# Layer norms of a four-layer graph kernel: centring and scaling on ScalarE, tile by tile, in place of VectorE

## Chip, cores and metric

The kernel runs on one core of a Trainium2 chip. The metric is the device time of one execution in microseconds (us), median of several runs. Profiles are taken in runs of their own, and they take longer: the profiled execution of the kernel before has a span of 7481.3 us, while its plain runs take 5338.69 us. Times inside a profile are therefore used for durations, order and waits, not as shares of the plain time.

## The reference, cut to what matters

Sixteen graphs (B = 16) of 1024 nodes with 64 features go through four layers, and each ends in a layer norm over the 64 features:

```python
def _layernorm(x, axis=-1, eps=1e-5):
    m = jnp.mean(x, axis=axis, keepdims=True)
    v = jnp.var(x, axis=axis, keepdims=True)
    return (x - m) / jnp.sqrt(v + eps)
...
x = _layernorm(x + _L0_gnn_ref(...))   # messages adj @ h, a small tanh MLP
x = _layernorm(x + _L1_gnn_ref(x, adj))  # messages by the row-normalised adjacency
x = _layernorm(x + _L2_gnn_ref(x, adj, nodemask, ...))  # quantiles over a thinned neighbour list, then a relu MLP
x = _layernorm(x + _L3_gnn_ref(x, adj, nodemask, ...))  # the same with other weights
```

So a norm is taken 16 x 4 = 64 times, each over a [128 partitions, 8 tiles, 64 features] float32 tile: 1024 nodes as 8 tiles (NT = 8) of 128 partitions, C = 64.

## The kernel before

The program is made of Python generators that emit instructions. For each graph b, `features` computes layers 0 and 1 (two norms), `lists` the neighbour lists, `ordered` an order of the nodes by list length. For each round k, `sort_round` sorts the gathered neighbour features of two graphs at once (graph k in layer 2, graph k-2 in layer 3), `fill` produces the last tile's neighbours by matmuls with one-hot matrices, and `finish` does the MLP and the norm of layers 2 and 3. The order on each engine is fixed when the program is built. A generator yields a number of microseconds, and it goes on when a clock has moved by that much. The clock is the time of VectorE, counted by a wrapper around its calls:

```python
class Metered:
    def __init__(self, engine):
        self.engine, self.us = engine, 0.0
    def __getattr__(self, name):
        ...
            self.us += 0.13 + size / (3840 if fast else 960)
            return call(*args, **kwargs)
...
    def settle(dst, y, chain):           # the layer norm: y in, dst out
        st = s.work.tile([P, 4, NT], F32, name=f"ln_st_{chain}", bufs=1)
        dve.reduce_sum(st[:, 0], y, axis=AX.X)
        dve.tensor_scalar(st[:, 1], st[:, 0], 1.0 / C, None, op0=ALU.mult)
        dve.tensor_sub(y, y, st[:, 1, :, None].to_broadcast([P, NT, C]))
        yield 2
        nc.scalar.activation(dst, y, AF.Square)
        yield 7
        dve.reduce_sum(st[:, 2], dst, axis=AX.X)
        yield 1
        nc.scalar.activation(st[:, 3], st[:, 2], AF.Sqrt, bias=eps, scale=1.0 / C)
        yield 6
        dve.reciprocal(st[:, 0], st[:, 3])
        dve.tensor_mul(dst, y, st[:, 0, :, None].to_broadcast([P, NT, C]))
```

Where the norm is called, and what follows it:

```python
    def features(b, e):                  # layers 0 and 1
        ...
        yield 8
        for h in range(NH):              # two halves
            ...                          # yields of 50 in each half
            dve.tensor_add(y[:, h * G : (h + 1) * G], pd, x_s[:, h * G : (h + 1) * G])
        dve.tensor_add(y, y, b02r[:, None, :].to_broadcast([P, NT, C]))
        yield from settle(x1[:, :, :C], y, "x")
        while b and not entries[b - 1].packed:
            yield 2
        near = s.sets.tile([P, NT, N], F16, name="near")
        for h in range(NH):
            ...  # matmuls pa <- adj, x1; near = adj > 0
        e.near = near                    # lists(b) starts from this
        ...
        yield from settle(x2, y, "x")
        ...
    def finish(b, e, layer, agg):        # layers 2 and 3
        ...
        yield from settle(xn, y, "m")
        yield 1
        ...
        for t in range(NT):
            put = nc.gpsimd.indirect_dma_start(...)   # one scatter a tile, table<-x3s or out<-agg
    ...
    def prepare():
        for b in range(B):
            while b > allowed[0] or (b and not entries[b - 1].taken):
                yield 2
            preparing[b] = [weave.add(features(b, entries[b]))]
            while b and not entries[b - 1].listed:
                yield 2
            preparing[b].append(weave.add(lists(b, entries[b])))
    ...
        for k in range(B + 2):
            allowed[0] = k + 2
            sort_round(k)
```

In `lists(b)` the flag `taken` is set after the last write of the tile `takes`, which is where `features(b + 1)` may start. The first instruction of `features` on VectorE sets a column of x1 to 1 (a MEMSET on x). The weighted sum over sorted neighbours already runs on ScalarE with a per-partition factor, one 128x64 tile at a time:

```python
                nc.scalar.activation(prods[:, m, i, :], got[:, m, slot_id, :], AF.Copy, scale=e.wts[:, t, i : i + 1])
```

The program also holds a general path for graphs whose lists are longer than usual, with a layer norm of its own. It doesn't run on these inputs and isn't changed.

Of the kernel before, what the change touches and what calls it, by code (L numbers as in the profile page):

```python
# [17 lines left out]
AF = mybir.ActivationFunctionType  # L18
ALU = mybir.AluOpType
AX = mybir.AxisListType  # L20

P = 128
# [190 lines left out]
def adj_resnorm_kernel(ctx: ExitStack, tc: tile.TileContext, x, adj_t, nodemask, w01, b01, w02, b02,  # L213
                       w21, b21, w22, b22, w31, b31, w32, b32, out):
    nc = tc.nc
    B, N, C = x.shape
    NT = N // P
# [4 lines left out]
    dve = Metered(nc.vector)  # L222
# [138 lines left out]
    def settle(dst, y, chain):  # L361

        st = s.work.tile([P, 4, NT], F32, name=f"ln_st_{chain}", bufs=1)
        dve.reduce_sum(st[:, 0], y, axis=AX.X)
        dve.tensor_scalar(st[:, 1], st[:, 0], 1.0 / C, None, op0=ALU.mult)
        dve.tensor_sub(y, y, st[:, 1, :, None].to_broadcast([P, NT, C]))
        yield 2
        nc.scalar.activation(dst, y, AF.Square)
        yield 7
        dve.reduce_sum(st[:, 2], dst, axis=AX.X)  # L370
        yield 1
        nc.scalar.activation(st[:, 3], st[:, 2], AF.Sqrt, bias=eps, scale=1.0 / C)
        yield 6
        dve.reciprocal(st[:, 0], st[:, 3])
        dve.tensor_mul(dst, y, st[:, 0, :, None].to_broadcast([P, NT, C]))

    def split(xc, parts, rest):

# [13 lines left out]
    def features(b, e):  # L392
# [18 lines left out]
        for h in range(NH):  # L411
# [26 lines left out]
# [5 lines that stand above are left out]
# [19 lines left out]
        x2 = s.feat.tile([P, NT, C], F32, name="x2", tag="x_s", bufs=1)  # L462
        dve.tensor_add(y, y, x1[:, :, :C])
        yield from settle(x2, y, "x")
        nc.sync.dma_start(table[0][b % 3][:N, :].rearrange("(t p) c -> p t c", p=P), x2)
        while b >= 2 and not entries[b - 2].filled[0]:
# [282 lines left out]
    def finish(b, e, layer, agg):  # L749
# [25 lines left out]
        dve.tensor_add(y, y, xc)  # L775
        xn = agg if layer else s.feat.tile([P, NT, C], F32, name="x3s", bufs=3)
        yield from settle(xn, y, "m")
        yield 1
        dst, rows = (out_rows_of, e.out_rows) if layer else (table[1][b % 3], e.rows)
# [447 lines left out]
```

## Time and profile before

| | |
|---|---|
| time, median of 3 runs | 5338.69 us (5337.18 to 5345.71) |
| span of the profiled execution | 7481.3 us |
| instructions | 107026 |
| instructions of VectorE / ScalarE | 9407 / 4644 |
| busy: TensorE / VectorE / ScalarE / GpSimd | 3981.8 / 4695.2 / 1972.5 / 3369.5 us |

In the profile DVE is VectorE, ACT is ScalarE, PE is the matrix engine and PEld its weight loads, POOL is GpSimd. A group of instructions has its line in the program (L207 is the wrapper through which most of VectorE's calls go, so these are told apart by their tiles), its tiles as output<-inputs, its shapes, its count, busy time, mean duration in ns, and the idle time of the engine before it with what ended that idle time. "remote" stands for a releaser that the trace doesn't name.

### The profile page before, as it was taken

The page shows a single profiled execution, that of the slowest core. Times are in us where ns is not written, and L with a number is a line of the kernel's source. Part 1 is how long each engine was busy: PE and PEld are TensorE (multiplying, and loading weights), DVE is VectorE, ACT ScalarE, POOL GpSimd, SP SyncE. Part 2 cuts the span into 40 slices and gives each one's busy share as a digit, 9 for nine tenths or more (in the row PEclk, how much of TensorE's full clock was granted, in tenths as well). Part 3 has the DMA queues.
Part 4 walks back from the last instruction along what each step waited for, and adds up shares of the span by engine and source line. Part 5 has one row for each costly group of instructions (what it writes and reads, how often), then busy time and mean ns, then how long its engine had stood idle before and what let it go on. Part 6 is the DMA issues. An engine that isn't in the chain of part 4 may idle for free.

```text
span 7481.3 us, 107026 instructions
## 1 busy us (share of the span) xinstructions
PE 3981.8 (53%) x43144; PEld 2843.2 (38%) x43144; DVE 4695.2 (63%) x9407; ACT 1972.5 (26%) x4644; POOL 3369.5 (45%) x3228
## 2 busy tenths in 40 slices
PE   7554566565645546565454655546565563533233
PEld 5333344443434334344243443434344342322232
DVE  2554567758648475675656657675665766558676
ACT  3130423332304132241412323142231413111111
POOL 0425245555533545444354544444545444554352
PEclk8675767676767667676676766666675766655555
DMA  3112111111111111111111111111111110100000
GB/s 83 41 33 46 32 41 39 44 43 41 42 37 30 30 38 39 40 39 42 22 39 30 41 41 34 43 28 29 41 38 45 27 40 14 21 18 15 12 19 10
DMA packets 420585, 259.11 MB, mean 35 GB/s; under 512 B 106590, under 2 KB 368878, under 8 KB 420078
## 3 DMA queue, kind: packets, MB, share of 16 engines
q0 software_dynamic: 102400, 105.06, 7.3%
q1 hardware_dynamic: 317678, 147.12, 7.1%
q8 instruction: 339, 5.55, 0.3%
q14 instruction: 168, 1.38, 0.1%
HBM read 239.37 MB, written 12.58 MB: 34 GB/s over the span
## 4 chain that ended last, share of the span: by engine, by line
DVE 33%; PE 29%; issue 24%; another core or an unknown queue 7%; ACT 3%; POOL 3%; DMA 1%; SPq 0%; DVEq 0%; POOLq 0%; ACTq 0%
DVE other L207 12%; PE pgk L348 10%; DVE got L207 6%; DVE got_s L207 6%; PE pk L592 6%; PE px L420 3%; PE pr L506 2%; POOL got_s L352 2%; PE pa L451 2%; DVE hot L207 2%; PE ordered_x L348 2%; DVE best L207 1%; DVE y_x L207 1%; DVE near L207 1%
## 5 line engine op out<-in xcount | busy, mean ns | idle before, releaser
L352 POOL DMA_INDIRECT got_s<-table,idx x2944 | 3090.2, 1050 | 3714.1 <-DVE other L207 1226.8
L348 PEld LDWEIGHTS <-hot 128*128 128x128 bf16 x24576 | 1141.3, 113 | 1992.0 <-issue 1660.9
L207 DVE TENSOR_SCALAR hot<-place 128x1024 bf16<-128x1024 f16 x1024 | 444.8, 435 | 1406.5 <-remote 1096.8
L348 PE MATMUL pgk<-x3p,hot 128*128 128x64 bf16 x12288 | 726.2, 219 | 865.6 <-issue 693.7
L348 PE MATMUL pgk<-x2p,hot 128*128 128x64 bf16 x12288 | 686.6, 213 | 739.9 <-issue 639.4
L592 PE MATMUL pk<-near,order 128*128 128x512 f16 x2048 | 585.4, 431 | 203.0 <-issue 186.2
L207 DVE TENSOR_TENSOR other<-got_s 128x512 f32<-128x512 f32 (+8 forms) x900 | 514.9, 583 | 12.3 <-DVE got_s L207 0.3
L207 DVE TENSOR_TENSOR got_s<-got_s 128x384 f32<-128x384 f32 (+7 forms) x918 | 490.6, 537 | 18.8
L506 PE MATMUL pr<-steps,near 128*128 128x512 bf16 x1536 | 429.2, 436 | 136.6 <-ACT junk L512 78.3
L737 ACT ACTIVATE got_s<-got_s,wts 128x64 f32<-128x64 f32 x1568 | 398.7, 335 | 290.1 <-DVE got_s L207 258.4
L451 PE MATMUL pa<-x,adj_r 128*128 128x65 f32 x2048 | 404.9, 367 | 118.1 <-issue 84.3
L451 PEld LDWEIGHTS pa<-x,adj_r 128*128 128x128 f32 x2048 | 385.2, 283 | 128.2 <-issue 93.0
L549 PE MATMUL pv<-minus_n,takes 128*128 128x128 bf16 x1024 | 237.7, 257 | 336.4 <-DVE takes L207 331.3
L207 DVE TENSOR_TENSOR got_s<-other 128x512 f32<-128x512 f32 (+8 forms) x774 | 408.0, 540 | 7.2
L592 PEld LDWEIGHTS <-order 128*128 128x128 bf16 x2048 | 208.3, 106 | 534.8 <-issue 365.5
L207 DVE MAX8 best<-code 128x8 f16<-128x1024 f16 x112 | 136.7, 1221 | 409.8 <-ACT code L603 383.5
L727 ACT COPY got<-pgk 128x512 f32<-128x512 f32 x128 | 74.7, 583 | 1125.7 <-remote 534.0
L207 DVE TENSOR_TENSOR other<-got 128x128 f32<-128x128 f32 (+5 forms) x270 | 233.1, 880 | 173.8 <-ACT got L727 165.3
L207 DVE TENSOR_TENSOR other<-other 128x128 f32<-128x128 f32 (+13 forms) x558 | 318.1, 570 | 14.8
L548 PE MATMUL pv<-scaled,near 128*128 128x128 f16 x1024 | 238.8, 258 | 156.2 <-ACT near L553 149.9
L512 ACT ACTIVATE junk<-pr,nb_st 128x1024 f16<-128x1024 f32 x256 | 282.3, 1109 | 149.1 <-PE pr L506 82.6
L549 PEld LDWEIGHTS <-takes 128*128 128x128 bf16 x1024 | 117.9, 115 | 515.7 <-DVE takes L207 355.4
(195 smaller groups left out, 6627.1 us busy)
## 6 DMA issues: line engine op xcount, KB each, us to landing
adj_r<-in_adj_dram SPq DMA_DIRECT2D x256, 512.0 KB
got_s<-table,idx POOLq DMA_INDIRECT x2944
x_s<-in_x_dram SPq DMA_DIRECT2D x16, 256.0 KB
table<-x SPq DMA_DIRECT2D x16, 256.0 KB
x<-table SPq DMA_DIRECT2D x16, 256.0 KB
table<-x3s,rows POOLq DMA_INDIRECT x128
out_dram<-agg,out_rows POOLq DMA_INDIRECT x128
table<-no_row SPq DMA_DIRECT2D x6, 0.2 KB
```

What stands on the lines that cost most here:

```text
L207: return call(*args, **kwargs)
L348: nc.tensor.matmul(dst, hot[:, c, :], parts[:, c, q, :], start=first and c + q == 0, stop=c == NT - 1 and q == 2)
L352: nc.gpsimd.indirect_dma_start(out=dst, out_offset=None, in_=tab, in_offset=bass.IndirectOffsetOnAxis(ap=rows, axis=0))
L420: nc.tensor.matmul(px[C:, q * P : (q + 1) * P], x_s[:, jt, :], adj[t][:, jt, :], start=jt == 0, stop=jt == NT - 1)
L451: nc.tensor.matmul(pa[:, q, :], adj[i][:, jt, :], x1[:, jt, :], start=jt == 0, stop=jt == NT - 1)
L506: nc.tensor.matmul(pr[:, h * HALF : (h + 1) * HALF], near[:, c, t * P : (t + 1) * P], steps[:, ONSET + h * HALF - c * P :][:, :HALF], star ...
L512: nc.scalar.activation(junk, prs[t - 1], AF.Sign, bias=lim[:, i, t - 1 : t], scale=-1.0, accum_out=cut_at[:, i, t - 1 : t])
L548: nc.tensor.matmul(pv[:, cols], near[:, c, rows], scaled[:, c, :], start=True, stop=False)
L549: nc.tensor.matmul(pv[:, cols], takes[:, c, rows], minus_n, start=False, stop=False)
L592: nc.tensor.matmul(cols, order[:, c, t * P : (t + 1) * P], left(c, slice(h * G, (h + 1) * G)), start=c == 0, stop=c == NT - 1)
L727: nc.scalar.copy(got[:, m, g : g + 8, :], pg)
L737: nc.scalar.activation(prods[:, m, i, :], got[:, m, slot_id, :], AF.Copy, scale=e.wts[:, t, i : i + 1])
```

## The change

Both passes of the norm that combine a whole tile with a per-row number leave VectorE. ScalarE does them instead, with one instruction for each of the 8 tiles: it adds minus the mean as a per-partition bias (Identity), and multiplies by the reciprocal deviation as a per-partition scale (Copy). VectorE keeps the two sums, the mean and the reciprocal. The purpose is to take work from VectorE and give it to an engine with more idle time. The yields are set anew: the wait before the second sum goes from 7 to 9, and a yield of 1 before and of 7 after the scaling are added.

```diff
         st = s.work.tile([P, 4, NT], F32, name=f"ln_st_{chain}", bufs=1)
         dve.reduce_sum(st[:, 0], y, axis=AX.X)
-        dve.tensor_scalar(st[:, 1], st[:, 0], 1.0 / C, None, op0=ALU.mult)
-        dve.tensor_sub(y, y, st[:, 1, :, None].to_broadcast([P, NT, C]))
+        dve.tensor_scalar(st[:, 1], st[:, 0], -1.0 / C, None, op0=ALU.mult)
         yield 2
+        for t in range(NT):
+            nc.scalar.activation(y[:, t, :], y[:, t, :], AF.Identity, bias=st[:, 1, t : t + 1])
         nc.scalar.activation(dst, y, AF.Square)
-        yield 7
+        yield 9
         dve.reduce_sum(st[:, 2], dst, axis=AX.X)
         yield 1
         nc.scalar.activation(st[:, 3], st[:, 2], AF.Sqrt, bias=eps, scale=1.0 / C)
         yield 6
         dve.reciprocal(st[:, 0], st[:, 3])
-        dve.tensor_mul(dst, y, st[:, 0, :, None].to_broadcast([P, NT, C]))
+        yield 1
+        for t in range(NT):
+            nc.scalar.activation(dst[:, t, :], y[:, t, :], AF.Copy, scale=st[:, 0, t : t + 1])
+        yield 7
```

## The prediction

> **What bounds the kernel now.** I began with the page's first part, the busy times:
>
> ```profile
> PE 3981.8 (53%) x43144; PEld 2843.2 (38%) x43144; DVE 4695.2 (63%) x9407; ACT 1972.5 (26%) x4644; POOL 3369.5 (45%) x3228
> ```
>
> The shares are of the profiled span of 7481.3 us. The plain run takes 5338.69 us. VectorE's durations hardly vary from instance to instance (691 to 694 ns for one form below), so I take its busy time to be the same in a plain run: 4695.2 / 5338.69 = 88%. No other engine comes near it by this reckoning except TensorE (75%, with ends that are modelled). Where are the other 5338.7 - 4695.2 = 643 us? I cut the profile into three stretches (columns after the window's length: busy time and instructions of PE, PEld, DVE, ACT, POOL, then granted clock, share of DMA, GB/s):
>
> ```profile
> 0.00:1015.00 1015.00, 579.61 (x5208) 408.36 (x5209) 474.38 (x1220) 275.27 (x528) 325.55 (x355) 0.69 0.19 46
> 1015.00:6356.00 5341.00, 2983.14 (x32582) 2125.19 (x32581) 3473.90 (x6594) 1520.14 (x3542) 2534.77 (x2383) 0.67 0.15 36
> 6356.00:7481.00 1125.00, 419.04 (x5356) 309.63 (x5356) 746.87 (x1595) 177.13 (x574) 509.20 (x491) 0.57 0.08 16
> ```
>
> In the first stretch, until three graphs are prepared, VectorE idles for 541 us; in the last, with nothing left to prepare, for 378. Both are waits on dependencies, part of which a plain run has too. If it keeps some two thirds of them (my guess), about 600 of the 643 idle us lie there, and in the middle VectorE is busy nearly throughout. In the profile it idles in the middle as well. The waits of VectorE between 2700 and 6310 us say on what:
>
> ```profile
> DVE hot L207 <- remote: 634.0, 53, 48.4
> DVE hot L207 <- PE pgk L348: 141.4, 53, 21.4
> DVE best L207 <- ACT code L603: 100.1, 7, 54.2
> ```
>
> `hot` is a one-hot matrix for the fill; its buffer is freed by a matmul, so these are waits on TensorE. TensorE's own largest wait in the whole profile is "issue" (1794.9 us before weight loads), which I read as mostly profiling's own cost, since the plain run is 2142 us shorter. None of these waits has anything to do with the norms. So the middle is bound by VectorE in a plain run, and VectorE's work there is what counts.
>
> **What the skill says.** The Trainium skill, "Perfetto Trace Analysis", section "Optimizing Scalar/DVE Operations": if VectorE is saturated, moving work to ScalarE may make sense; both pay a fixed cost per instruction. "ScalarE: Activation LUTs", section "What ACT_TABLE_LOAD costs": an activation with immediates takes 186 ns + 0.833 ns per element, each per-partition pointer operand adds about 93 ns, and back-to-back activations overlap by about 93 ns. For 64 elements that is 186 + 53 + 93 = 332 ns, one every 239 ns. The trace has the same operation, the weighing with a per-partition factor, and agrees: mean 335 ns, and the median distance from one start to the next is 239 ns. "ScalarE: Activation LUTs", section "Table sets: the hidden batching unit": copy and identity are in every table set, so they cause no table load. The trace agrees for Copy and Square: of 52 loads, 26 stand at the square root and 25 at tanh, one at another line. Identity isn't in the trace.
>
> **The change part by part.** The groups by form, with mean ns after the busy time:
>
> ```profile
> L207 DVE TENSOR_TENSOR y_x<-y_x,ln_st_x 128x512 f32<-128x512 f32 x32 | 22.2, 693 | 1.1
> L207 DVE TENSOR_TENSOR y_m<-y_m,ln_st_m 128x512 f32<-128x512 f32 x32 | 22.2, 693 | 1.1
> L207 DVE TENSOR_TENSOR x<-y_x,ln_st_x 128x512 f32<-128x512 f32 x32 | 22.1, 692 | 1.1
> L207 DVE TENSOR_TENSOR agg<-y_m,ln_st_m 128x512 f32<-128x512 f32 x16 | 11.1, 692 | 0.5
> L207 DVE TENSOR_TENSOR x3s<-y_m,ln_st_m 128x512 f32<-128x512 f32 x16 | 11.1, 692 | 0.6
> ...
> L737 ACT ACTIVATE got_s<-got_s,wts 128x64 f32<-128x64 f32 x1568 | 398.7, 335 | 290.1 <-DVE got_s L207 258.4 <-DVE hot L207 23.8 <-issue 4.0
> ```
>
> Removed from VectorE: 32 + 32 + 32 + 16 + 16 = 128 instructions, 22.2 + 22.2 + 22.1 + 11.1 + 11.1 = 88.7 us busy, and 4.4 us of gaps before them (34 ns each): 93 us, or 1.45 us a norm. A full round has four norms: 5.8 us of its 312 us of VectorE work (distance between the same points of neighbouring rounds, added up in VectorE's busy time).
>
> Added to ScalarE: 64 x 16 = 1024 instructions at 239 ns, 245 us. It then has some 2217 us, 42% of a plain run. In a full round that is 15 us more, on an engine with about 124 us of work in such a round. It is not the bound.
>
> Latency of a norm. The last one of the program, where nothing else is in the way (VectorE and ScalarE lines of the timeline: start, duration):
>
> ```profile
> 7462.42 0.69 DVE L207 TENSOR_REDUCE ln_st_m<-y_m 128x8 f32<-128x512 f32 x1
> 7463.14 0.17 DVE L207 TENSOR_SCALAR ln_st_m<-ln_st_m 128x8 f32<-128x8 f32 x1
> 7463.35 0.69 DVE L207 TENSOR_TENSOR y_m<-y_m,ln_st_m 128x512 f32<-128x512 f32 x1
> 7464.07 0.63 ACT L368 ACTIVATE agg<-y_m 128x512 f32<-128x512 f32 x1 [5.62 <-DVE y_m L207]
> 7464.73 0.69 DVE L207 TENSOR_REDUCE ln_st_m<-agg 128x8 f32<-128x512 f32 x1 [0.70 <-ACT agg L368]
> 7465.46 0.30 ACT L372 ACTIVATE ln_st_m<-ln_st_m,eps 128x8 f32<-128x8 f32 x1 [0.76 <-DVE ln_st_m L207]
> 7465.79 0.20 DVE L207 RECIPROCAL ln_st_m<-ln_st_m 128x8 f32<-128x8 f32 x1 [0.37 <-ACT ln_st_m L372]
> 7466.03 0.69 DVE L207 TENSOR_TENSOR agg<-y_m,ln_st_m 128x512 f32<-128x512 f32 x1
> ```
>
> Each 0.72 us step (0.69 and a gap) becomes eight activations, 7 x 0.239 + 0.335 = 2.0 us. So a norm gets 2 x (2.0 - 0.72) = 2.6 us longer where it is waited for: at the end of the program once (+2.6), and at its start, where VectorE idles and the first graphs' two norms are in the chain: three graphs, at most 3 x 2 x 2.6 = 15 us, of which I count 10.
>
> Lead of the preparation. The yields of a norm go from 2 + 7 + 1 + 6 = 16 to 2 + 9 + 1 + 6 + 1 + 7 = 26. The first norm of `features` lies in a loop: `taken` of graph b, features of b + 1 up to near, lists of b + 1, its `taken`. From the MEMSET that opens `features` to the next such MEMSET, in VectorE's busy time, the trace gives 285, 299 and 290 us for the early graphs and 312 for the late ones. Early, it follows the last `takes` at once (start 2323.94, MEMSET 2326.48); late, it comes 16 us after (4984.86, 5000.83). So early on the loop itself sets the pace (about 290), it gains on the rounds (312), and from the ninth graph or so the limit of two rounds' lead holds it. After the change the loop takes about 290 + 10 (yields) + 2 (lag of two more steps) - 1.45 = 301, the rounds 312 - 5.8 = 306. The preparation still keeps up, but only just: its lead stays small for the whole run rather than growing.
>
> Sum: of the 64 norms I leave out ten as not in a stretch that VectorE bounds (the first three graphs' six in `features` and two in layer 2, the last two of the program). 54 x 1.45 = -78. Start +10, end +2.6. For the smaller lead, with more waits on late lists and on ScalarE's queue, +18 (a guess: 1.5 us for each of 12 rounds). Together -47 us, 5338.7 - 47 = 5291, say 5290.
>
> **The rivals.** (1) TensorE is the bound in the middle: then the 78 us turn into longer waits of `hot`, and the time is 5340 to 5355. For it speaks that `hot` is VectorE's largest wait in the profile; against it that this profile slows TensorE and that the plain run leaves at most some tens of us of idle time in the middle. (2) The preparation loop becomes the bound: if the loop takes 5 us more than a round, 13 x 5 = 65 us are lost again, and the time is about 5340 to 5390. For it speaks the narrow gap of 301 to 306; against it that both are worked out from the same clock. (3) ScalarE's order: its queue is in order, and the scaling can stand behind a copy that waits for a matmul (waits of 10 us and more on TensorE are in its list of waits, 520.9 us in all on pgk alone). VectorE's multiply didn't stand behind those. Then PE's pa matmuls or the scatters come late; the added yield of 7 should cover most of it: +0 to +40. (4) Everything converts: -93 + 5, 5251.
>
> **Range and chances.** Between (4) and the mixed cases: 5230 to 5350. Faster by over 2% would be below 5232, more than the removed work: 0.05. Slower by over 2% would be above 5445, for which the loop would have to lose 13 x 12 us or more: 0.05. Within 2%: 0.90.
>
> **What would show it.** Right: the five groups above are gone, 9407 - 128 = 9279 instructions on VectorE, its busy time about 89 us less; 1024 more activations at 335 ns, one every 239; no more table loads at Identity; the late rounds about 306 us of VectorE's time apart, with the MEMSET right behind the last `takes` throughout. Wrong: VectorE waits for ScalarE at ln_st for more than a few us in many norms; the sort waits for gathers or for the fill more often; VectorE's busy time falls but its idle time before `hot` grows as much; or a VectorE that is not the bound at all, with a time that stays.

## The result, and the profile after

The changed kernel takes 5320.66 us (median of 4 runs, 5318.06 to 5321.83), the kernel before beside it 5342.08 us (5337.18 to 5345.71). The ratio is 0.996, with a 95% interval of 0.9943 to 0.9977. So the change gives 21 us, where the prediction said 48, with the time inside the range of 5230 to 5350. A second comparison gave 0.9961 (0.9946 to 0.9976).

Some of the comparisons, and the profile on which the prediction was built, fell in a condition in which the kernel before takes 7430 to 7624 us in place of 5333 to 5347; the matmuls of the fill then follow each other at about 91 ns in the mean, otherwise at about 51 (distances of up to some 2 us counted), and as one chip showed both, the words "fast chip" and "slow chip" in the expectations below mean this condition. Every ratio here is taken within one comparison. Below, "at 5340" and "at 7480" name the condition by the time of the kernel before.

A new profile of the kernel before, at 5340, has these busy times (first part of the page):

```profile
PE 3434.8 (64%) x43144; PEld 2655.5 (50%) x43144; DVE 4690.2 (88%) x9407; ACT 1969.4 (37%) x4644; POOL 3666.5 (69%) x3228
```

The changed kernel beside it, in the same comparison:

```profile
PE 3377.1 (64%) x43144; PEld 2582.0 (49%) x43144; DVE 4605.8 (87%) x9279; ACT 2208.6 (42%) x5662; POOL 3668.3 (69%) x3228
```

The spans are 5331.5 and 5317.1 us. VectorE has the 128 instructions fewer and 84.4 us less to do. Its idle time, span less busy time, went from 641.3 to 711.3 us: 70 us up. So the work did go, and most of it came back as waiting. ScalarE's 239 us more come with the new groups, of which four are (group, count, busy time, mean ns, idle time before them):

```profile
L368 ACT ACTIVATE y_x<-y_x,ln_st_x 128x64 f32<-128x64 f32 x256 | 64.6, 335 | 315.2 <-DVE ln_st_x L207 315.2
L368 ACT ACTIVATE y_m<-y_m,ln_st_m 128x64 f32<-128x64 f32 x256 | 64.6, 334 | 145.3 <-DVE ln_st_m L207 145.3
L378 ACT ACTIVATE x<-y_x,ln_st_x 128x64 f32<-128x64 f32 x256 | 64.5, 334 | 148.7 <-DVE ln_st_x L207 101.2 <-DVE nb_st L207 47.4
L378 ACT ACTIVATE x3s<-y_m,ln_st_m 128x64 f32<-128x64 f32 x128 | 32.2, 335 | 12.8 <-DVE ln_st_m L207 12.5
```

Where did the waiting come back? Cut into start, middle and end at the same times (columns as in the prediction), the kernel before at 5340:

```profile
0.00:1150.00 1150.00, 772.67 (x8599) 583.82 (x8600) 830.90 (x1907) 429.20 (x889) 588.86 (x579) 0.76 0.24 58
1150.00:4170.00 3020.00, 2086.23 (x26535) 1615.41 (x26532) 2825.95 (x5361) 1239.17 (x2890) 2296.56 (x1967) 0.76 0.23 53
```

and the changed kernel:

```profile
0.00:1150.00 1150.00, 738.29 (x8339) 559.56 (x8340) 783.46 (x1817) 450.41 (x1034) 566.72 (x557) 0.76 0.23 57
1150.00:4170.00 3020.00, 2070.71 (x26595) 1572.58 (x26591) 2805.56 (x5347) 1392.69 (x3549) 2322.11 (x1988) 0.76 0.23 53
```

In the start VectorE works 783.5 us of the 1150 rather than 830.9. In the middle it idles for 214 rather than 194 us. By the rounds (a round ends with VectorE's last sum from the tail tile `got` into `agg`): the first two end at 387 and 695 us before and at 385 and 695 us after, so nothing is lost up to there. The third ends at 1076 before and at 1099 after. The fourth makes up for that (it ends at 1414 and 1413), the fifth loses it again (1716 and 1747). The waits of VectorE between 700 and 1100 us, in the third round, name what was lost there. The kernel before has

```profile
DVE best L207 <- ACT code L603: 10.1, 3, 6.9
...
DVE near L207 <- DMA adj_r<-in_adj_dram: 0.8, 1, 0.8
```

and the changed kernel

```profile
DVE near L207 <- DMA adj_r<-in_adj_dram: 33.7, 1, 33.7
DVE y_m L207 <- PE pd L775: 12.2, 1, 12.2
```

A single instruction on `near`, which compares a block of the adjacency with zero, waits 33.7 us for its load. The program fixes VectorE's order, so the sorting that stands behind this instruction waits too. Neither the norm nor ScalarE is part of this wait. Late rounds, on the other hand, do what the change is for: the last three before the tail take 310.3 to 310.5 us before and 303.5 to 304.1 after.

The fifth round has no such wait. In it VectorE waits for the fill: before, once for 3.5 us, and after the change above all in these places:

```profile
DVE hot L207 <- PE pgk L348: 20.7, 6, 6.9
DVE other L207 <- ACT got L731: 10.2, 1, 10.2
```

Over the whole program the waits show both. Of VectorE's waits in the kernel before, these are

```profile
DVE other L207 <- ACT got L727: 102.9, 14, 10.7
...
DVE near L207 <- DMA adj_r<-in_adj_dram: 42.8, 5, 32.1
DVE hot L207 <- PE pgk L348: 42.5, 34, 5.2
DVE other L207 <- DMA got_s<-table,idx: 33.8, 1, 33.8
DVE y_m L207 <- PE pd L771: 32.7, 5, 13.0
```

and in the changed kernel

```profile
DVE near L207 <- DMA adj_r<-in_adj_dram: 84.1, 5, 39.9
DVE hot L207 <- PE pgk L348: 82.8, 51, 6.9
DVE other L207 <- ACT got L731: 64.3, 14, 10.2
DVE y_m L207 <- PE pd L775: 50.8, 12, 12.2
...
DVE other L207 <- issue: 28.8, 1, 28.8
```

Of the 70 us, 41 are waits of `near`. `hot` waits 40 us more for matmuls of the fill, but `other` waits 39 us less for the copy `got` of what the fill made, so the two together hardly change (145.4 and 147.1 us): the fill is waited for at another place, not longer. The MLP's sum `y_m` waits 18 us more.

Why is the load late? The timeline of the loads' queue (start, time from the first to the last of the merged entries, line, transfer, count) in the kernel before:

```profile
656.27 126.31 SPq L403 DMA_DIRECT2D adj_r<-in_adj_dram  x13
815.84 0.37 SPq L795 DMA_DIRECT2D x<-table  x1
816.31 3.64 SPq L403 DMA_DIRECT2D adj_r<-in_adj_dram  x3
```

and in the changed kernel:

```profile
656.62 113.92 SPq L407 DMA_DIRECT2D adj_r<-in_adj_dram  x9
816.27 0.37 SPq L799 DMA_DIRECT2D x<-table  x1
816.74 19.27 SPq L407 DMA_DIRECT2D adj_r<-in_adj_dram  x7
```

The entry x<-table is the read-back of x3: `read_back`, a generator that `finish` starts after the norm of layer 2, and which the prediction never looked at. It waits until the scatters of x3s have landed (45.7 us in the changed kernel), and loads behind it on the queue wait with it. It goes at 816 us in both kernels. What differs is its place: before, 13 of a graph's 16 loads stood ahead of it, after the change 9. GpSimd's timeline in the changed kernel shows why it goes at 816 us and not earlier (start, duration, what ended the idle time before it):

```profile
803.82 0.94 POOL L352 DMA_INDIRECT got_s<-table,idx  x1 [0.30 <-DMA got_s<-table,idx]
805.07 1.00 POOL L785 DMA_INDIRECT table<-x3s,rows  x1 [0.30 <-DMA got_s<-table,idx]
...
814.02 0.97 POOL L785 DMA_INDIRECT table<-x3s,rows  x1 [0.30 <-issue]
```

The scatters stand behind a run of gathers that began at 728 us. ScalarE had x3s ready by 765.5 us:

```profile
763.50 2.02 ACT L378 ACTIVATE x3s<-y_m,ln_st_m 128x64 f32<-128x64 f32 x8
```

So x3s lay there for 40 us, then the scatters took 10 us, the read-back went, the load behind it went, and `near` started at 821.7 us.

### The profile page after: what moved, and what is told of

It is laid out like the page before. It is cut to its first block, busy times and chain, and to the rows that moved or that the text cites. A ratio compares the mean times of both kernels' runs of the same rounds, so it can differ in the third digit from the quotient of the medians.

```text
span 5320.1 us, 107953 instructions
## 1 busy us (share of the span) xinstructions
PE 3372.3 (63%) x43084; PEld 2586.5 (49%) x43144; DVE 4606.9 (87%) x9279; ACT 2208.3 (42%) x5662; POOL 3671.4 (69%) x3228
## 4 chain that ended last, share of the span: by engine, by line
DVE 69%; PE 14%; POOL 5%; issue 5%; ACT 3%; DMA 3%; DVEq 0%; POOLq 0%; SPq 0%; ACTq 0%
DVE other L207 22%; DVE got_s L207 17%; DVE got L207 10%; DVE hot L207 5%; POOL got_s L352 4%; DVE best L207 4%; PE pgk L348 3%; PE pk L596 3%; PE pa L455 3%; DMA got_s<-table,idx 2%; DVE less L207 2%; PE px L424 1%; PE ordered_x L348 1%; DVE y_m L207 1%; DVE y_x L207 1%
## 5 line engine op out<-in xcount | busy, mean ns | idle before, releaser
L352 POOL DMA_INDIRECT got_s<-table,idx x2944 | 3351.9, 1139 | 1419.5 <-issue 770.8
L348 PEld LDWEIGHTS <-hot 128*128 128x128 bf16 x24576 | 997.8, 110 | 682.5 <-DVE hot L207 568.2
L348 PE MATMUL pgk<-x3p,hot 128*128 128x64 bf16 x12288 | 553.4, 211 | 253.3 <-DVE hot L207 252.7
L348 PE MATMUL pgk<-x2p,hot 128*128 128x64 bf16 x12288 | 550.1, 211 | 213.4 <-DVE hot L207 202.5
L207 DVE TENSOR_TENSOR other<-got_s 128x512 f32<-128x512 f32 (+8 forms) x900 | 516.0, 584 | 49.2 <-issue 28.8
L596 PE MATMUL pk<-near,order 128*128 128x512 f16 x2048 | 473.7, 385 | 20.6 <-ACT code L607 13.9
L510 PEld LDWEIGHTS <-near 128*128 128x128 f16 x1536 | 169.6, 113 | 556.4 <-issue 447.0
L762 PE MATMUL pt<-ident,agg 128*64 128x128 f32 x256 | 52.8, 344 | 488.1 <-DVE agg L207 462.9
L424 PE MATMUL px<-adj_r,x_s 128*64 128x128 f32 x2048 | 270.4, 290 | 13.4 <-DMA adj_r<-in_adj_dram 11.4
L741 ACT ACTIVATE got<-got,wts 128x64 f32<-128x64 f32 x672 | 164.7, 335 | 270.6 <-DVE got L207 270.6
L762 PEld LDWEIGHTS pt<-ident,agg 128*64 128x64 f32 x256 | 29.5, 135 | 500.6 <-DVE agg L207 459.6
```

Source lines behind the costliest of these rows:

```text
L348: nc.tensor.matmul(dst, hot[:, c, :], parts[:, c, q, :], start=first and c + q == 0, stop=c == NT - 1 and q == 2)
L352: nc.gpsimd.indirect_dma_start(out=dst, out_offset=None, in_=tab, in_offset=bass.IndirectOffsetOnAxis(ap=rows, axis=0))
L424: nc.tensor.matmul(px[C:, q * P : (q + 1) * P], x_s[:, jt, :], adj[t][:, jt, :], start=jt == 0, stop=jt == NT - 1)
L510: nc.tensor.matmul(pr[:, h * HALF : (h + 1) * HALF], near[:, c, t * P : (t + 1) * P], steps[:, ONSET + h * HALF - c * P :][:, :HALF], star ...
L596: nc.tensor.matmul(cols, order[:, c, t * P : (t + 1) * P], left(c, slice(h * G, (h + 1) * G)), start=c == 0, stop=c == NT - 1)
L762: nc.tensor.transpose(pt[:C, q * P : (q + 1) * P], agg[:, h * G + q, :], ident)
```

## The experiments

The theory when they began (A): VectorE is the bound, its time does come through, and the missing half is lost at the start and the end. The rival (B): another engine shares the bound in the middle. A third (C) grew out of the traces: the change moves what it doesn't touch, the order on the load queue. The fourth (D) is that the longer lead costs, or that ScalarE's passes do.

**The kernel before again.** No edit. One measurement is at 7480, one at 5340; the latter is the profile used above.

> The kernel before once more, for a profile that isn't stretched as its first one (span 7481 us) was. All theories: span near its plain time, 5337 to 5347 us; VectorE busy about 4695 us. Theory A (VectorE sets the pace, the missing half is lost at the start and the end): a late round takes 309 to 311 us against 303.8 after the change, and the start and the end are some 30 us shorter than after the change. Theory B (another engine shares the bound in the middle): a late round takes about 305 us, with more idle time of VectorE than after the change, and start and end are alike.

Measured: 7508.43 us, VectorE busy 4695.3 us.

> The kernel before once more. The chips differ: it took 5340 us on one and 7480 us on another, where matmuls of the fill follow each other at 91 ns in the mean (after the change, on the faster chip: 49 ns). If this is a fast chip: VectorE busy 4695 us of about 5340, and theory A wants late rounds of 309 to 311 us (303.8 after the change), with a start and an end some 30 us shorter than after the change; theory B wants late rounds of about 305 us. If it is a slow one: again 7450 to 7520 us.

Measured: 5333.27 us, span 5331.5, VectorE busy 4690.2; late rounds 310.3 us. That is A's number for the late rounds, but only half of A's claim: start and end are not 30 us shorter than after the change, the loss begins in the third round. The two profiles together also show that VectorE's busy time doesn't depend on the condition (4695.3 and 4690.2).

**Both passes left out, and given to nobody.** What leaves a norm in this kernel is the square of its input, and centring and scaling are not computed.

```diff
-        dve.tensor_sub(y, y, st[:, 1, :, None].to_broadcast([P, NT, C]))
...
-        dve.tensor_mul(dst, y, st[:, 0, :, None].to_broadcast([P, NT, C]))
```

> Both passes left out and given to nobody, yields as before (what leaves a norm is then the square of its input). Theory A: the middle gives 54 x 1.45 = 78 us and start and end some more: 5245 to 5270 us. Theory B: TensorE or the order of the gathers takes over, and most of the 93 us turn into waits: 5305 to 5325 us.

Measured at 7480: 7366.92 against 7479.84 us, 0.9834 (0.9807 to 0.9861). The expected times were written for 5340 and don't apply.

> Both passes left out, yields as before. On a fast chip: theory A (VectorE's time converts) 5245 to 5270 us; theory B (most of it turns into waits) 5305 to 5325 us. On a slow chip 1.7% below the kernel before, as measured there.

Measured at 5340: 5281.00 against 5339.26 us, 0.9887 (0.9872 to 0.9902). That is 58 us, between both theories. Its waits in the third round:

```profile
DVE near L207 <- DMA adj_r<-in_adj_dram: 42.5, 1, 42.5
DVE best L207 <- ACT code L601: 8.9, 3, 6.9
```

With ScalarE untouched, no yield changed and nothing but VectorE's work gone, the same wait is there, with 11 loads ahead of the read-back. 58 us gained and up to 42 that this one wait takes make about 100 us; the removed work was put at 93, and without the passes the norms in the chain at the start are shorter too (the first round ends at 371 us, before at 387). So apart from the wait VectorE's time seems to have come through, and nothing is left for B to explain at 5340. That is worked out, not shown: the passes left out together with a free load queue were not measured.

**The yields alone.** VectorE does both passes as before.

```diff
-        yield 7
+        yield 9
...
         dve.reciprocal(st[:, 0], st[:, 3])
+        yield 1
         dve.tensor_mul(dst, y, st[:, 0, :, None].to_broadcast([P, NT, C]))
+        yield 7
```

> The kernel before with the yields of the changed kernel (9 for 7, 1 and 7 more), VectorE still does both passes. If the longer lead is what eats the gain: 5360 to 5375 us. If the yields cost nothing: 5335 to 5350 us.

Measured at 7480: 7677.72 us, 1.0255 (1.0230 to 1.0280), far more than expected.

> The kernel before with the yields of the changed one. On a fast chip: 5360 to 5375 us if the longer lead eats the gain, 5335 to 5350 us if it costs nothing there because TensorE has time to spare. On a slow chip 2.5% above the kernel before, as measured there.

Measured at 5340: 5374.23 us, 1.0059 (1.0045 to 1.0073), 35 us slower, at the number of "the longer lead eats the gain". The trace has 28.8 us in the same wait of `near` in the third round (9 loads ahead of the read-back), so a part of the price of the lead is a price of the queue. How large a part this run doesn't show: the third round takes 25 us more than in the kernel before, the fourth 19 less, the fifth 18 more.

**The changed kernel beside them.** No edit.

> The changed kernel itself on this chip. On a fast chip 0.994 to 0.998 of before, as measured. On a slow chip: yields alone cost 2.5% there and leaving the passes out gives 1.7%, the sum is about +1%: 7520 to 7580 us against 7480.

Measured at 5340: 5319.75 us, 0.9961. Leaving out (-58) and the yields (+35) add up to -23, the kernel has -20. That leaves 3 us for ScalarE's passes, but both parts hold the same wait once each and the kernel holds it once, so the small remainder proves little.

**ScalarE's passes with the old yields.** The changed kernel with 7 for 9 and without the yields around the scaling. All four measurements are at 7480 or above; how this version does at 5340 is not known.

```diff
-        yield 9
+        yield 7
...
-        yield 1
         for t in range(NT):
             nc.scalar.activation(dst[:, t, :], y[:, t, :], AF.Copy, scale=st[:, 0, t : t + 1])
-        yield 7
```

> The changed kernel with the yields of the kernel before (7, and none around the scaling). If the longer lead is what eats the gain: 5285 to 5305 us. If ScalarE's longer passes themselves do (in its queue or in waits for it): 5315 to 5335 us, with more waits of VectorE and TensorE for ScalarE at the norms.

> The changed kernel with the yields of the kernel before. Its loads of the adjacency stand in the kernel before's order around the read-back of x3 (13 ahead of it, 3 behind, in the third round; after the change 9 and 7). On a fast chip (before 5340 us): if the order on the load queue is what eats the gain, the third round has no wait of near on adj_r and the time is 5245 to 5275 us; if ScalarE's passes themselves cost, 5290 to 5320 us. On a slow chip (7480 us): 1.003 to 1.008 of before, as measured there.

> The changed kernel with the yields of the kernel before, for a fast chip: 13 loads ahead of the read-back as before, so 5245 to 5275 us if the order on the load queue eats the gain; 5290 to 5320 us if ScalarE's passes do. On a slow chip (7480 us) 1.005 to 1.007 of before, as measured there twice.

> The changed kernel with the yields of the kernel before, in the condition in which before takes 5340 us: its load queue has 13 loads ahead of the read-back, as before, so the third round has no wait of near on adj_r and the time is 5260 to 5290 us; 5300 to 5325 us if ScalarE's passes without a longer lead make VectorE or TensorE wait for them. Where before takes 7480 us: 1.005 to 1.007 of it, as measured there twice.

Measured: 1.0055 (1.0031 to 1.0080), 1.0072 (1.0047 to 1.0098), 1.0051 (1.0033 to 1.0069) at 7480, and 1.0132 (1.0109 to 1.0155) where the kernel before took 7612 us. So at 7480 the passes on ScalarE cost: leaving them out gives 1.7%, giving them to ScalarE loses 0.5 to 1.3%. Where they cost it there was not followed further. It isn't C: no trace at 7480 has a wait of `near` of more than 6 us in the second or third round.

**The read-back later.** An attempt at C that moved nothing.

```diff
+        yield 50
         x3 = s.feat.tile([P, NT, C], F32, name="x3", bufs=1)
         nc.sync.dma_start(x3, src[:N, :].rearrange("(t p) c -> p t c", p=P))
-        yield 60
+        yield 10
```

> The changed kernel with its own yields, the read-back of x3 put into the load queue 50 us later and used after 10 instead of 60 us: only the order on the load queue moves. On a fast chip: if that order eats the gain, the wait of near on adj_r (39.9 and 33.7 us in the second and third round) goes, and the time is 5255 to 5290 us; if it doesn't, 5315 to 5325 us.

> The kernel before with the same later read-back. It has one such wait (32 us, second round). On a fast chip: 5305 to 5330 us if the order on the load queue counts, 5335 to 5350 us if not.

> ScalarE's passes, the yields of the kernel before, and the later read-back. On a fast chip: the best of the four if waits in the load queue are the loss, 5215 to 5250 us; if they aren't, the same as with the old yields alone.

Measured at 7480 (kernel before 7481.97 us): with the change 1.0066 (1.0046 to 1.0085), without it 0.9956 (0.9942 to 0.9971), with the old yields 1.0005 (0.9987 to 1.0023). Inconclusive for C, by its condition and by itself: in the third round the trace still has 9 loads ahead of the read-back and 7 behind with the change, and 13 and 3 without. The program lists only VectorE, ScalarE and TensorE as engines whose order it sets itself (`manual_schedule`); the load queue isn't among them, and a yield ahead of the read-back doesn't move it. Other edits did (11 loads ahead with the passes left out, 9 with the yields alone); what decides there was not followed. Why the kernel before and the one with the old yields take 0.4 and 0.7% less with this edit than without it stays open.

**The read-back issued by GpSimd.** This takes it out of the loads' queue for good. It stands right behind the scatters for which it waits.

```diff
-        nc.sync.dma_start(x3, src[:N, :].rearrange("(t p) c -> p t c", p=P))
+        nc.gpsimd.dma_start(x3, src[:N, :].rearrange("(t p) c -> p t c", p=P))
```

> The changed kernel with the read-back of x3 issued by GpSimd, so that no load of the adjacency can stand behind it. On a fast chip (before 5340, after 5320 us): if that queue is what eats the gain, the waits of near on adj_r in the second and third round (39.9 and 33.7 us) go and the time is 5250 to 5285 us; if the waits only move, 5310 to 5325 us. On a slow chip no more than 1% either way.

> The kernel before with the same move. On a fast chip it loses one such wait (32 us in the second round): 5305 to 5325 us if that wait counts, 5335 to 5345 us if the start is held by something else anyway.

Measured at 7480 (kernel before 7490.82 us): 1.0062 (1.0043 to 1.0082) with the change, 0.9979 (0.9965 to 0.9992) without it. The changed kernel by itself has no time at 7480 to set beside the first.

> The changed kernel with the read-back of x3 issued by GpSimd, once more, for a fast chip (before 5340, after 5320 us): if the load queue is what eats the gain, the waits of near on adj_r in the second and third round (39.9 and 33.7 us) go and the time is 5250 to 5285 us; if the waits only move elsewhere, 5310 to 5325 us. On a slow chip 1.006 of before, as measured there.

Measured at 5340: 5288.32 against 5339.41 us, 0.9900 (0.9883 to 0.9916). The change now gives 51 us rather than 20. The loads of the third round, then VectorE's two largest waits from 700 to 1100 us:

```profile
655.44 143.30 SPq L407 DMA_DIRECT2D adj_r<-in_adj_dram  x16
824.54 0.37 SPq L469 DMA_DIRECT2D table<-x  x1
```

```profile
DVE y_m L207 <- PE pd L775: 12.2, 1, 12.2
DVE key_c L207 <- ACT junk L574: 6.3, 1, 6.3
```

All 16 loads go without the read-back between them, `near` doesn't wait, and the round ends at 1066 us, 33 us sooner. The other waits of that stretch are as they were, to 0.2 us, but for one of 1.4 us that is new. The upper end of the expectation is just missed (5285), for a reason worth seeing: in the second round the move gains nothing. There `near` had waited 39.9 us and the sort, later, 28.8 (a wait whose releaser the trace doesn't name, where the kernel before waits 33.8 us for gathers); now the sort waits 69.9 us for its gathers alone:

```profile
DVE hot L207 <- PE pgk L348: 73.8, 47, 7.2
DVE other L207 <- DMA got_s<-table,idx: 71.3, 2, 69.9
DVE other L207 <- ACT got L731: 66.8, 14, 10.2
```

A wait is only worth its length where nothing else waits behind it. The kernel before has the 32.1 us wait of `near` in its second round alone, so by this it would gain next to nothing from the same move; at 5340 that wasn't measured.

**Old yields and GpSimd's read-back together.**

> ScalarE's passes, the yields of the kernel before, and the read-back of x3 issued by GpSimd. Where before takes 5340 us: if the longer lead is worth nothing once the load queue is free, about the 5288 us of the changed kernel with that move, within 8 us; if the lead keeps VectorE and TensorE from waiting for ScalarE, 5300 to 5330 us; if the lead itself costs, 5245 to 5275 us. Where before takes 7480 us or more: 1.00 to 1.01 of it.

Measured at 5340: 5269.38 against 5340.32 us, 0.9869 (0.9853 to 0.9886), the best of all. With the queue free, the longer lead itself costs 0.31% (0.9900 against 0.9869; with intervals of 0.16% either way that is clear of noise, but not by much). Its middle stretch:

```profile
1150.00:4170.00 3020.00, 2109.87 (x27151) 1629.08 (x27189) 2826.52 (x5396) 1424.85 (x3591) 2335.72 (x2017) 0.76 0.24 55
```

VectorE idles for 193.5 of 3020 us there, as in the kernel before (194.0), while the changed kernel with GpSimd's read-back idles for 210.5. In that stretch the largest change between the two is the wait of `hot` on the fill's matmuls, 48.0 us with the new yields and 29.3 with the old. But `other` waits for the fill's copy 51.6 us with the new yields and 61.1 with the old, so 9 of the 17 us remain. Over the whole program the version with the old yields has

```profile
DVE other L207 <- ACT got L729: 82.2, 13, 12.1
...
DVE hot L207 <- PE pgk L348: 43.6, 36, 5.9
```

together 125.8 us against 140.6 with the new ones. By the rounds, the new yields make the fourth shorter and the fifth longer: these take 314 to 319 and 319 to 334 us in the three versions at 5340 that have them, 325 to 337 and 302 to 303 in the three that don't. At the end of the fifth round the two versions with GpSimd's read-back are level (1708 and 1706 us). The sixth then takes 310 us with the new yields and 294 with the old, and from there the new ones stay 15 to 29 us behind. How the yields bring the waits for the fill about was not followed.

## Why the prediction was wrong

Its direction and its range held, and so did the half of its mechanism that makes the gain: VectorE's work is worth its time. What takes a part of the gain away again was mis-sized, and came by a path that the prediction didn't have. Its 48 us were 21. Step by step:

- **VectorE is the bound of the middle.** Right at 5340: 2825.95 of 3020 us busy, and the version with the old yields and a free load queue gains 71 us. Two readings on the way were wrong. The 2142 us between profile and plain time were put down to profiling, there and where the metric is described; a profile at 5340 has a span of 5331.5 us for a run of 5333.3, so profiling costs nothing here, and the first profile showed another condition. And "about 600 of the 643 idle us" were placed at start and end; it is 641.3 - 194.0 = 447.
- **Removed: 93 us.** Right: 9279 instructions, 84.4 us less busy time. Late rounds got 6.4 to 6.8 us shorter, predicted 5.8.
- **Added to ScalarE.** Right: 334 to 335 ns each, 2208.6 us busy, predicted 2217. There are 45 table loads at the square root and tanh (51 before), and none at Identity. This is what the Trainium skill, "ScalarE: Activation LUTs", section "Table sets: the hidden batching unit", says of cheap functions, and the trace now shows it for Identity too.
- **Latency, +10 at the start and +2.6 at the end.** Too large: the first round ends 2 us sooner than before and the second 1 us later. At the end the norm takes 5.6 us from its first sum to the first scatter, before 4.6: 1.0 us more. The scatter of a tile needs that tile's scaling alone, so it starts behind the first of eight activations:

```profile
5302.14 2.02 ACT L378 ACTIVATE agg<-y_m,ln_st_m 128x64 f32<-128x64 f32 x8 [0.27 <-DVE ln_st_m L207]
5302.76 0.96 POOL L785 DMA_INDIRECT out_dram<-agg,out_rows  x1 [71.28 <-ACT agg L378]
```

- **Lead: the loop takes 301, the rounds 306.** Close: from MEMSET to MEMSET 284 to 306 us of VectorE's time from the fifth graph on, 307 to 308 late. (These are durations added up, as in the prediction. Neighbouring instructions overlap a little in the trace, so 308 fit into a round of 304.) The late MEMSET follows the last `takes` after 3.4 us, before after 15.4.
- **"For the smaller lead ... +18 (a guess: 1.5 us for each of 12 rounds)".** This is the term that failed; it was mis-sized and its main part misplaced. It was spread thin over the rounds and tied to late lists and ScalarE's queue. What stands in its place is, first, one wait in one round, in a queue that the prediction didn't look at: taking it away brought 31 us (51 less 20). Second, the longer yields by themselves: 17 us by the ratios (0.31%), 20 by the gains (71 less 51). The prediction counted on them to cover waits for ScalarE. Together that is some 50 against 18. That these parts and the 20 us of the change add up to 71 is no test, as they are differences of the same gains.
- **The rest of the sum.** The version without both, old yields and read-back by GpSimd, gains 71 us, and the sum without the failed term is -78 + 10 + 2.6 = -65. That is close in part by luck: in this version the first two rounds end 1 us sooner than before rather than 10 later, and the rounds from the third to the last bring 68 us (the last ends at 5227, before at 5296) rather than 78.

Of the rivals, (1), TensorE as the bound, doesn't hold at 5340: the waits of `hot` did grow by 40 us, but all waits for the fill together by 2, and the time didn't stay. (2), the loop as the bound, isn't seen either: the late rounds are 6.4 to 6.8 us shorter, and VectorE waits no longer in them (12.8 us in the fourteenth round, before 15.1). (3), ScalarE's order, is not seen at the norms: the waits of VectorE for ScalarE at `ln_st` stay below 3 us each.

## What to carry to other kernels

Where instruction order follows from a modelled clock, taking work away or setting a yield anew can move later instructions, also on queues that the change doesn't touch. Compare the order on each queue before and after, the load queue above all: a transfer that waits for something far upstream holds up each load behind it, so give it a queue in which what it waits for stands directly ahead of it. And retime leads with care: here, with the load queue free, the old yields with the new engine took 5269 us and the new ones 5288.

## What the runs showed of the hardware that was not expected

VectorE's busy time is the same to 0.1% in both conditions (4690.2 and 4695.3 us), while TensorE's matmuls of the fill follow each other at 51 and at 91 ns. And the sign of a change can depend on the condition: the changed kernel with GpSimd's read-back takes 1.0062 of the kernel before at 7480 and 0.9900 at 5340. The granted clock was 0.73 at 5340 and 0.66 at 7480; whether it is cause or consequence the runs don't show.
